# The second and the last mixture of experts: another way to choose, to invert the choice, and to add the last rows

## The chip, the cores and the metric

The kernel runs on one core of one Trainium2 chip. The time is the device time of one execution in microseconds (us); the profile is one further execution, with a trace of every instruction. TensorE is PE in the rows (PEld its weight loads), VectorE DVE, ScalarE ACT, GpSimd POOL, SyncE SP. All data is float32.

## The reference

The network adds twelve blocks, one after the other, to x (16 sequences of 64 tokens, 256 wide, so 1024 tokens): four layers, each a cross attention, a mixer and a feed-forward block. Two of the feed-forward blocks, here called mixtures, send each token to 2 of 8 experts. The last of them, cut to what matters:

```python
    logits = xt @ wg
    scores = jax.nn.softmax(logits, axis=-1)
    topv, topi = jax.lax.top_k(scores, K)                    # K = 2 of E = 8
    topv = topv / jnp.sum(topv, axis=-1, keepdims=True)
    masks = jax.nn.one_hot(topi.T, E, dtype=jnp.int32)
    locs = jnp.cumsum(masks.reshape(K * N, E), axis=0) - 1   # place within the expert
    ...
    valid = pos < capacity                                   # capacity = 256 rows an expert
    h = jax.nn.relu(jnp.einsum('ecm,emh->ech', disp, w1) + b1[:, None, :])
    y = jnp.einsum('ech,ehm->ecm', h, w2) + b2[:, None, :]
    out = jnp.sum(gate[..., None] * y[topi, pos_c], axis=1)
```

The hidden width is 1024. The second mixture (layer 1) chooses in the same way, has gelu in place of relu, adds 1e-9 to the sum of the two scores and has no capacity: every choice is kept. x in front of each block is its layer norm.

## The kernel before

X, the residual, stays in the core's memory as 8 tiles of 128 tokens by 256. `BLOCKS` calls the twelve blocks in order; `ffn1` (line 2438) is the second mixture, `ffn3` (line 2553) the last and the end of the program. `ffn0` and `ffn2` are mixtures of another kind, in which every expert sees every token.

Both `ffn1` and `ffn3` have three parts. The **front**: `norm_T` (layer norm, then transposes into xnT), the normed tokens written to a table d_x in HBM, `gate_logits` (line 2151, 16 matmuls into pgate), `softmax8`, and `ranks` (line 2178), which compares each of a token's 8 scores with each other one, 512 comparisons a partition, and counts. `choices` (line 2245) makes from the ranks one-hot tables oh of the first and second choice, and counts, by a scan and matmuls with a triangle and with ones (pq), which place each choice has within its expert. `slots` (line 2268) inverts this: for each row g*128+r of the experts' packed rows it finds the token that comes there and its weight. inb says for each of 16 groups of choices (8 tiles by 2) in which of 128 lanes each stands, val holds in which block it is times the token's number or its weight, and 16 matmuls into pi sum them up:

```python
        for j in range(J):
            self.mm(pi[:, : 2 * NG], inb[:, j], val[:, j], j == 0, j == J - 1)
```

Seven small DVE operations then make src (the row to fetch), to (the row to send to) and weight. `add_down_bias` (line 2190) adds to X the experts' output biases, weighted: it transposes the weights (pc), copies them (combT) and multiplies 9 rows by the biases downb, a matmul for each tile (pb).

The **blocks of rows**: 23 blocks of 128 rows in `ffn1` (each with its expert's weights, up and down, fetched by an indirect DMA whose row numbers are whose), 8 of 256 in `ffn3`. `take` fetches a block's tokens from d_x (xg) by an indirect DMA on the POOL queue; `expert` (line 2332) transposes them (pxg), copies (xT), multiplies (pu), applies the activation (hT), multiplies again (pd), weights the result (y) and sends it by an indirect DMA, also on the POOL queue, into a table d_y of 2048 rows, a row for each choice.

The **end**: `add_sent` (line 2371) reads d_y back in 8 DMAs of 256 KB (yk), four on SP's queue and four on ACT's. Each waits for all sends; two additions a tile put them into X. After `ffn3`, `network` writes X out in 8 DMAs on SP's queue (line 2705).

The order of instructions on each engine comes from a scheduler that goes by the program's order and by what is ready in its own estimate; `set_order(True)` with `queue` and `mm` ties instructions of an engine to the order in which they are written. In the mixtures nothing is tied before the change. Each engine works through its own instructions in order, and an indirect DMA takes its place in POOL's.

## Time and profile before

| | us |
|---|---|
| median of 3 runs | 3125.39 (3124.48 to 3126.11) |
| the profiled execution | 3139.76 |
| its span, first to last instruction | 3138.1 |
| PE busy | 2942.0 (94%) |
| DVE busy | 1966.8 (63%) |
| ACT busy | 1340.0 (43%) |
| POOL busy | 712.7 (23%) |
| last logit matmul to first expert matmul, `ffn1` | 1393.5 to 1426.5 |
| last y to the last addition to X, `ffn1` | 1612.5 to 1628.5 |
| last logit matmul to first expert matmul, `ffn3` | 2968.8 to 3001.8 |
| last y to the last addition to X, `ffn3` | 3121.5 to 3135.0 |

A row of a timeline gives the start, the duration, the engine, the line, the operation, the tiles written and read, how many, and in brackets how long the engine stood idle before it and what ended that. A row of groups gives all instructions of a kind: busy time, the mean of one in ns, and the idle time before them. Most lines of operations recorded through a queue are 72, and those of matmuls 188, so tiles are named rather than lines. A float32 matmul stands as two passes, each with a weight load. A window's row ends in the granted clock of TensorE (1 is full), the busy share of the DMA engines and GB/s.

### The profile page before, as it was taken

The numbers are of one execution on the slowest core, as the hardware profiler recorded it, in microseconds if no ns is written. First come the engines' busy times: TensorE is split into PE (matmuls) and PEld (weight loads), VectorE is DVE, ScalarE is ACT, GpSimd is POOL, SyncE is SP. The second block draws the span as 40 slices with busy tenths as digits, with TensorE's granted clock in tenths as the row PEclk, the third lists the DMA queues.
The fourth block names the chain that finished last, engine by engine and source line by source line (L and its number), as shares of the span: only waits on it lengthen the run. The fifth ranks groups of instructions, "written<-read, shape, count | busy, mean of one in ns | idle before, by whom it ended". The sixth has DMA issues, their size and how long they took to land.

```text
span 3138.1 us, 64791 instructions
## 1 busy us (share of the span) xinstructions
PE 2942.0 (94%) x27232; PEld 1792.9 (57%) x27232; DVE 1966.8 (63%) x4085; ACT 1340.0 (43%) x3013; POOL 712.7 (23%) x780
## 2 busy tenths in 40 slices
PE   8999999898999999979978999997999899998797
PEld 4666666565555554458854555544655454546676
DVE  6888886523766656961127777768874667775511
ACT  3555554412554441003325444449851255554211
POOL 1000002400210001014410100026761454541131
PEclk9999999999999999968989999998999999999789
DMA  2001000014223313017751222201111111110233
GB/s 75 32 32 32 22 29 12 18 34 109 63 79 93 99 45 82 21 55 270 296 180 52 72 72 77 65 13 44 41 57 34 60 67 55 70 44 15 95 111 120
DMA packets 73796, 223.05 MB, mean 71 GB/s; under 512 B 17457, under 2 KB 28580, under 8 KB 66594
## 3 DMA queue, kind: packets, MB, share of 16 engines
q1 hardware_dynamic: 45936, 113.99, 11.9%
q0 software_dynamic: 21840, 99.39, 9.4%
q10 hardware_dynamic: 5730, 5.53, 0.6%
q8 instruction: 215, 3.52, 0.5%
q14 instruction: 75, 0.61, 0.1%
HBM read 210.00 MB, written 12.66 MB: 71 GB/s over the span
## 4 chain that ended last, share of the span: by engine, by line
PE 81%; DVE 7%; issue 5%; POOL 2%; ACT 2%; DMA 2%; SPq 0%; POOLq 0%; ACTq 0%; DVEq 0%
PE pss L188 15%; PE o L188 13%; PE psp L188 5%; PE pu L188 5%; PE pkv L188 5%; PE pd L188 5%; PE py L188 4%; PE pst L191 4%; PE psc L188 3%; PE po L188 2%; PE pb L191 2%; PE psq L188 2%; PE psi L188 1%; PE psy L188 1%; PE pg L188 1%
## 5 line engine op out<-in xcount | busy, mean ns | idle before, releaser
L188 PE MATMUL pss<-cT,qw 128*32 128x256 f32 x8192 | 367.7, 385 | 18.8 <-ACT pr L72 18.6
L72 DVE TENSOR_REDUCE nm<-pss 128x2 f32<-128x512 f32 (+1 forms) x384 | 309.5, 862 | 83.9 <-PE pss L188 83.9
L188 PE MATMUL o<-pT,cx 128*64 128x512 f32 (+3 forms) x1088 | 351.7, 576 | 0.0
L72 ACT ACTIVATE pr<-pss,nmm 128x256 f32<-128x256 f32 x512 | 234.8, 485 | 162.2 <-DVE nmm L72 162.2
L188 PEld LDWEIGHTS pss<-cT,qw 128*32 128x32 f32 x8192 | 203.2, 109 | 148.6 <-ACT pr L72 26.3
L188 PEld LDWEIGHTS o<-pT,cx 128*64 128x64 f32 (+1 forms) x1088 | 134.2, 163 | 188.4 <-issue 161.8
L205 POOL TENSOR_SCALAR rs<-mv 128x8 f32<-128x8 f32 (+3 forms) x50 | 9.7, 195 | 1006.3 <-DVE mv L221 534.0
L72 ACT ACTIVATE pr<-pr,sm 128x256 f32<-128x256 f32 x256 | 109.1, 497 | 203.1 <-DVE sm L72 203.1
L188 PE MATMUL pkv<-wx,cT 128*128 128x512 f32 (+1 forms) x512 | 193.3, 631 | 0.6 <-issue 0.6
L72 DVE TENSOR_SCALAR pr<-pr,sm 128x256 f32<-128x256 f32 (+1 forms) x384 | 170.1, 485 | 6.6
L72 DVE TENSOR_TENSOR_SCAN h<-dA,pb 128x512 f32<-128x512 f32 x128 | 154.7, 1217 | 16.0 <-PE pb L191 9.6
L1495 POOL TENSOR_TENSOR h<-h,cb 128x1024 f32<-128x1024 f32 x64 | 151.5, 2369 | 53.6 <-DVE h L72 51.2
L2355 DVE TENSOR_SCALAR y<-pd,row 128x256 f32<-128x256 f32 x39 | 18.9, 484 | 223.2 <-PE pd L188 192.7
L72 DVE STREAM_TRANSPOSE pT<-pr 128x1024 f32<-128x1024 f32 x128 | 151.8, 1224 | 2.2
L188 PE MATMUL pd<-wd,hT 128*128 128x256 f32 x656 | 149.3, 382 | 2.9 <-DVE hT L2543 1.4
L72 ACT ACTIVATE pr<-pss,nm 128x1024 f32<-128x1024 f32 x128 | 142.7, 1115 | 11.3 <-DVE nm L72 8.7
L191 PE MATMUL pst<-ident,pr 128*128 128x128 f32 x1024 | 141.5, 281 | 5.8 <-DVE sm L72 1.9
L191 PEld LDWEIGHTS pst<-ident,pr 128*128 128x128 f32 x1024 | 110.1, 141 | 62.1 <-ACT pT L72 26.5
L72 ACT COPY pT<-pst 128x512 f32<-128x512 f32 x128 | 75.0, 586 | 164.2 <-PE pst L191 164.2
L188 PEld LDWEIGHTS pd<-wd,hT 128*128 128x128 f32 x656 | 123.1, 190 | 31.4 <-DVE hT L2543 6.2
L188 PEld LDWEIGHTS pkv<-wx,cT 128*128 128x128 f32 (+1 forms) x512 | 64.5, 189 | 118.4 <-issue 92.2
L1669 POOL TENSOR_TENSOR rnk<-rnk,mhalf 128x8 f32<-128x8 f32 (+1 forms) x84 | 130.1, 1549 | 7.0
(525 smaller groups left out, 5795.5 us busy)
## 6 DMA issues: line engine op xcount, KB each, us to landing
cT<-in_ctxT SPq DMA_DIRECT2D x32, 768.0 KB, 4.3
cx<-in_ctxP SPq DMA_DIRECT2D x32, 768.0 KB, 4.2
cT<-in_ctxT SPq DMA_DIRECT2D x32, 512.0 KB, 4.1
cT<-in_ctxT SPq DMA_DIRECT2D x64, 256.0 KB, 5.3
offb<-d_off SPq DMA_DIRECT2D x16, 576.0 KB, 3.7
cb<-d_C SPq DMA_DIRECT2D x16, 512.0 KB, 4.1
wu<-in_L_ffn_w POOLq DMA_DIRECT2D x8, 1024.0 KB
wd<-in_L_ffn_w POOLq DMA_DIRECT2D x8, 1024.0 KB
```

Of the source, the lines that this page charges most:

```text
L72: ins = getattr(self.engine, op)(*args, **kwargs)
L188: self.in_order(self.nc.tensor.matmul(out, lhsT=lhsT, rhs=rhs, start=start, stop=stop))
L191: self.in_order(self.nc.tensor.transpose(out, in_, self.ident))
L205: nc.gpsimd.tensor_scalar(t[:p, :n], in_, scale, eps, ALU.mult, ALU.add)
L1495: nc.gpsimd.tensor_tensor(hs[i], hs[i], cbs[hf, g], ALU.mult)
L1669: nc.gpsimd.tensor_tensor(r, r, self.mhalf[:, : n * H], ALU.pow)
L2355: nc.vector.tensor_scalar(y[:, i, :], po[:, i * D : (i + 1) * D], weight[:, g + i : g + i + 1], None, ALU.mult)
```

## The change

It has four parts, in both mixtures.

- `choose` takes the place of `gate_logits`, `softmax8`, `ranks` and `choices`: the first choice by the maximum of the logits, the second by the maximum of what is left, ties to the lower expert through a falling row 8 to 1. The exponentials are not divided by their sum; `over_both` divides at the end. A one-element Exp stands ahead of the logits.
- `slots`: val becomes the loaded operand, 32 columns wide, and inb the moving one; output j goes to the 32 rows 32*(j%4), and a matmul with fold adds the four parts up. The token's row comes first (pi), its fetch is issued, and only then the products for the weight and for the row to send to are made on POOL and multiplied (pw). The experts' biases are multiplied in four groups of rows (pc, pb; downb now stands four times, at rows 0, 32, 64 and 96). Several operations move from DVE to POOL, and the order is tied.
- `add_sent`: the last block of rows is not sent. The read-back comes ahead of the last block in the program, on SP's queue alone, and waits for the other sends; POOL adds the two halves. hits is 1 where a token is the one that a row of the last block belongs to; 8 matmuls with it add the last y. d_y is now cleared in `ffn1` too (2 MB), and the last expert of `ffn3` is worked in two blocks of 128.
- the output DMAs alternate between SP and ACT.

The instructions' order on each engine is otherwise that of before. On POOL in `ffn1` it is now: comb, comb, up, down, at, up, val, down, up, xg, gate, xg, val, val, down, xg; in `ffn3`: kept, kept, comb, at, val, xg, xg, gate, xg, val, val, xg. On PE: pq, pn (`ffn1`), pc, pi, the first fold product, pb, pw, pxg, two fold products, pu. On DVE the first addition of a yk stands ahead of the last y.

```diff
-        self.downb = self.const.tile([9, 3, D], F32, name="downb")
-        nc.scalar.dma_start(out=self.downb, in_=a["downb"])
+        self.downb = self.const.tile([P, 3, D], F32, name="downb")
+        for q in range(4):
+            nc.scalar.dma_start(out=self.downb[32 * q : 32 * q + 9], in_=a["downb"])
...
+    def choose(self, wg, d_x, one, mid):
...
+        nc.scalar.activation(best[:, 3, 0:1], self.xn[:, 0, 0:1], AF.Exp)
...
+        self.set_order(True)
...
+        dve.tensor_reduce(best[:, 0], pg3, AX.X, ALU.max)
+        dve.tensor_tensor(d, pg3, bc(best[:, 0], 2, 8), ALU.subtract)
+        nc.scalar.activation(p, d, AF.Exp)
+
+        dve.scalar_tensor_tensor(w, d, 0.0, falling, ALU.is_ge, ALU.mult)
+        dve.tensor_reduce(best[:, 1], w, AX.X, ALU.max)
+        dve.tensor_tensor(by_t[:, 0], w, bc(best[:, 1], 2, 8), ALU.is_equal)
+        dve.scalar_tensor_tensor(d, by_t[:, 0], -4.0, p, ALU.mult, ALU.add)
+        dve.tensor_reduce(best[:, 2], d, AX.X, ALU.max)
+        dve.tensor_tensor(w, d, bc(best[:, 2], 2, 8), ALU.is_equal)
+        dve.tensor_tensor(w, w, falling, ALU.mult)
+        dve.tensor_reduce(best[:, 1], w, AX.X, ALU.max)
+        dve.tensor_tensor(by_t[:, 1], w, bc(best[:, 1], 2, 8), ALU.is_equal)
...
+        pool.tensor_tensor(at[:, :, :NG], at[:, :, :NG], at[:, :, 1:], ALU.subtract)
+        spot = self.spot.rearrange("p k t -> p (k t)")
+        pool.tensor_tensor(val[:, 0, :, :NG], at[:, :, :NG], bc(spot, 2, NG), ALU.mult)
...
+        def inverted(ps, k):
+            for j in range(J):
+                q = j % 4
+                self.mm(ps[32 * q : 32 * q + 32, :], val[:, k, j, :], inb[:, j], j < 4, j >= J - 4)
...
+        inverted(pi[:, :P], 0)
+        rows = one.tile([P, 3, P], F32, name="rows")
+        dve.tensor_copy(rows[:, 0], pi[:, :P])
+        pf = mid.tile([P, 512], F32, tag="m", name="pf")
+        self.mm(pf[:, :32], rows[:, 0], self.fold)
+        src, to = (one.tile([P, NG], I32, name=f"at{k}") for k in range(2))
+        dve.tensor_copy(src, pf[:, :NG])
+        got = taken(src)
+
+        pool.tensor_tensor(gate, gate, bc(r, 1, 2), ALU.mult)
+        pool.tensor_tensor(val[:, 1, :, :NG], at[:, :, :NG], bc(gate.rearrange("p k t -> p (k t)"), 2, NG), ALU.mult)
+        pool.tensor_tensor(val[:, 2, :, :NG], at[:, :, :NG], bc(self.token, 2, NG), ALU.mult)
...
+            for q in range(4):
+                rg = slice(32 * q, 32 * q + 9)
+                self.mm(pb[q // 2][:, q % 2, k, :], cT[rg, k, :], self.downb[rg, i, :])
+        pw = mid.tile([P, 2, P], F32, tag="m", name="pw")
+        for k in range(2):
+            inverted(pw[:, k, :], 1 + k)
+        act.copy(rows[:, 1:], pw)
+        for k in range(2):
+            self.mm(pf[:, 32 + 32 * k : 64 + 32 * k], rows[:, 1 + k], self.fold)
...
+    def add_sent(self, d_y, sent, last, src, g, row, one, pool, mid):
...
+        nc.vector.tensor_copy(own, src[:, g : g + 1])
+        nc.vector.tensor_scalar(hits, row, own, None, ALU.is_equal)
...
+            ins = nc.sync.dma_start(out=yk, in_=d_y.rearrange("(k t p) d -> t p k d", t=NT, p=P)[t])
             for other in sent:
                 self.tc.add_manual_dep(ins.ins, other, sync, reason="sent rows")
+            nc.gpsimd.tensor_tensor(yk[:, 0], yk[:, 0], yk[:, 1], ALU.add)
+            yks.append(yk)
+        y = last()
+        for t in range(NT):
+            nc.vector.tensor_tensor(self.X[:, t, :], self.X[:, t, :], yks[t][:, 0], ALU.add)
+        for t in range(NT):
+            ps = mid.tile([P, 512], F32, tag="m", name="py")
+            self.mm(ps[:, :D], hits[:, t * P : (t + 1) * P], y[:, 0, :])
+            nc.vector.tensor_tensor(self.X[:, t, :], self.X[:, t, :], ps[:, :D], ALU.add)
...
-        tc.nc.sync.dma_start(out=out[t * P : (t + 1) * P, :], in_=n.X[:, t, :])
+        (tc.nc.sync, tc.nc.scalar)[t % 2].dma_start(out=out[t * P : (t + 1) * P, :], in_=n.X[:, t, :])
```

## The prediction

> **What bounds the kernel now.** I read the clock and span first (one core, mean granted TensorE clock 0.952), then the chain of work that ended last: TensorE holds 81% of it. So only stretches in which TensorE has little to do can be shortened by this change. The view of stretches, cut to the fronts and ends of the second mixture (ffn1, rows 1 and 2) and the last (ffn3, rows 3 and 4), shows them. Columns: stretch, length, busy time of PE, PEld, DVE, ACT, POOL, granted clock, DMA share, GB/s.
>
> ```profile
> 1389.00:1426.00 37.00, 22.00 (x88) 18.00 (x87) 20.20 (x64) 3.41 (x4) 9.73 (x10) 0.53 0.48 171
> 1612.00:1632.00 20.00, 0.44 (x2) 0.04 (x1) 8.81 (x28) 0.00 (x0) 2.23 (x3) 0.61 0.47 145
> 2965.00:3002.00 37.00, 22.42 (x97) 18.48 (x98) 19.51 (x59) 0.84 (x2) 7.28 (x8) 0.54 0.44 135
> 3121.00:3138.00 17.00, 0.48 (x3) 0.07 (x1) 6.30 (x17) 0.00 (x0) 0.98 (x1) 0.63 0.55 188
> ```
>
> In all, 111 us, and in none of them the experts' weights are multiplied. The timeline of the last mixture's front tells what follows what (start, length, engine; x32 means 16 matmuls, since each f32 matmul stands as two passes):
>
> ```profile
> 2968.81 0.23 DVE L2157 COPY s<-pgate 128x64 f32<-128x64 f32 x1 [2.85 <-PE pgate L188]
> ...
> 2970.62 0.69 DVE L2184 TENSOR_TENSOR gt<-s 128x512 f32<-128x512 f32 x1
> ...
> 2979.46 2.50 DVE L2296 TENSOR_TENSOR inb<-sl,lane 128x512 f32<-128x512 f32 x4
> ...
> 2982.68 7.04 PE L188 MATMUL pi<-val,inb 128*128 128x32 f32 x32 [6.57 <-DVE val L2304]
> ...
> 2990.84 1.08 POOL L2324 DMA_INDIRECT xg<-L_ffnx,at  x1 [21.03 <-DVE at L2314]
> ...
> 2992.81 7.16 PE L188 MATMUL pb<-downb,combT 9*128 9x256 f32 x16 [1.40 <-DVE combT L2198]
> ...
> 3001.80 9.14 PE L188 MATMUL pu<-xT,wu 128*128 128x256 f32 x32 [0.78 <-DVE xT L2341]
> ```
>
> Logits end at 2968.8, the first expert matmul (pu) starts at 3001.8: 33.0 us of a serial chain. In ffn1 the same chain goes from 1393.5 to 1426.5, also 33.0. The end of ffn1, from its timeline:
>
> ```profile
> 1612.48 0.48 DVE L2355 TENSOR_SCALAR y<-pd,row 128x256 f32<-128x256 f32 x1 [7.91 <-PE pd L188]
> 1613.24 0.98 POOL L2358 DMA_INDIRECT L_ffny<-y,at  x1 [7.39 <-DVE y L2355]
> ...
> 1615.78 2.23 SPq L2377 DMA_DIRECT2D yk<-L_ffny  x4
> ...
> 1621.52 1.22 DVE L2384 TENSOR_TENSOR X<-X,yk 128x256 f32<-128x256 f32 x3 [5.68 <-DMA yk<-L_ffny]
> ```
>
> The last y waits for its send, the sends for the read-back, the read-back for the sums; X is whole at 1628.5, 16.0 us after that y. In ffn3 it is 3121.5 to 3135.0, with the output's own 3.1 us behind it.
>
> **The change, step by step.** Times count from the logits' end.
>
> *Choice.* The copy, softmax and pairwise ranks (five 0.69 us operations on 512 elements) go; eleven DVE operations on 64 elements at 0.26 (row s<-pgate and its neighbours, with the gap), the scan (0.45) and prev (0.30) stay on the path: 3.6 us. Before, prev ended 6.5 later in ffn3 and 7.8 in ffn1, where an activation table load of 1.28 us stood in the chain; the new tiny Exp on xn makes it early, while ScalarE idles. Gain 2.9 and 4.2. In ffn1 15 instead of 8 logit matmuls now stand behind the last transposes; at the 0.18 us a pass of that row's cold part this ends them 1 to 2.6 us later: -1.5.
>
> *Inversion (pi).* Before, 16 matmuls load 128 columns and move 32 or 46: 7.06 us. After, val (32 columns) is loaded and inb moves, four column groups side by side. The nearest row is pss in the attention, 128x32 loads, 8192 passes in 367.7 us, 45 ns each at 256 columns; half of those use two row groups as well (64 passes in 1.96 us, 31 ns), which leaves 59 ns for the plain kind, against 0.23 us for a full-width pass (pd, 16 in 3.72). At half clock and half the columns that is 59 ns again: 32 passes, 1.9 us. Here a rule has to be weighed. These two stretches are pi and pb in ffn1:
>
> ```profile
> 1411.00:1418.00 7.00, 6.79 (x32) 6.79 (x32) 0.16 (x1) 1.28 (x1) 0.53 (x1) 0.50 0.89 362
> 1418.00:1425.00 7.00, 7.00 (x18) 5.19 (x17) 3.77 (x14) 0.00 (x0) 4.38 (x5) 0.50 0.33 87
> ```
>
> The granted clock is 0.50 in both, though PE is busy for all 14 us. The Trainium skill, "TensorE: Matmul & The Clock Gate", Part 1, lets about 3.4 us of sustained work restore full clock; by it the new pi, pb and pw would run mostly at full clock and take about half of the 7.7 us I give them, some 3 us more gain per mixture. The row decides: thin products left the clock low, so I price all of the front at half clock. Its page "TensorEngine Tiling (Array Packing)", under Key Properties, says that changing the tiling mode drains TensorE; the front now changes it about five times. No row shows a price; the attention changes modes with no idle time in front, so between 0 and 0.5 us in all, taken as 0.
>
> *New work on POOL.* The subtraction at and the three val products move to GpSimd, beside comb. Nearest rows, and the issue costs that stand between them on this in-order queue:
>
> ```profile
> L1095 POOL TENSOR_TENSOR tapp<-tapp,tapb 128x256 f32<-128x256 f32 x16 | 11.7, 730 | 70.1 <-ACT tapp L72 69.0 <-DVE tapb L72 1.1
> L1016 POOL TENSOR_TENSOR xd<-xt,dt 128x512 f32<-128x512 f32 x8 | 10.4, 1298 | 9.6 <-ACT xt L72 9.5
> ```
> ```profile
> 1407.04 1.10 POOL L2488 DMA_INDIRECT up<-in_L_ffn_up,whose  x1 [12.45 <-DVE whose L2480]
> 1408.44 1.45 POOL L2488 DMA_INDIRECT down<-in_L_ffn_down,whose  x1 [0.30 <-issue]
> 1410.20 1.32 POOL L2488 DMA_INDIRECT up<-in_L_ffn_up,whose  x1 [0.30 <-issue]
> ```
>
> 368 elements (ffn1) take 0.98 by interpolation, 256 (ffn3) 0.74; a gather issue is 1.0 to 1.45 plus 0.30. The rule against this: "GPSIMD Engine Reference", 4.1, puts elementwise work on VectorE because GpSimd is about twice as slow with two inputs, and section 7 adds 50% for reads whose step is over 8 bytes (at is read beside 24-wide rows, spot and gate as broadcasts). DVE's own val rows were 0.53 (ffn1) and 0.42, so row and rule agree on the factor; with the surcharge five POOL operations cost about 2.5 us more in ffn1 and 1.5 in ffn3. I take the rows and keep the surcharge for the range.
>
> *ffn3 front.* After prev (3.6): oh, place, slots, low 3.35 us and inb 2.5, so 5.85; before 6.6. POOL is free and has val by then, so pi runs with inb and ends 0.6 later (before 7.9 after inb). Copy 0.29, fold product 0.4, conversion 0.17, gaps: src 1.0 later, the first gather issue at 3.6+7.8. Three gathers (1.25 each), gate 0.2, and two val products bring POOL to 13.4; pw, 64 passes, 3.8 us from the first of them at 12.6, to 16.4; only then pxg (1.1), two fold products (0.8), pu at 18.3. So 21.9 instead of 33.0: +11.1. Row-packed pb (16 passes, about 2 us), two 1.2 us additions to X and hits (0.69) lie under the POOL stretch; without it they would cost 3 us.
>
> *ffn1 front.* Here the POOL queue is in the way. After prev, pn, nine small operations to whose (4.0), place, sums and reciprocal: inb would be whole at 9.75. But POOL stands comb (needs the reciprocal, 5.5), up, down, at, up, val in that order: val comes at 11.8. pi ends at 13.7, src 14.7, gather 14.8 (behind a second down and up), gate, gather, val twice to 19.6, pw to 22.3, pxg and folds, pu at 23.8. Before, pu was 25.2 after prev. Gain 4.2-1.5+1.4: +4.1.
>
> *Ends.* The last block's y is no longer sent: eight products with the one-hot hits (2 passes of 0.23 each, 3.7 us) add it. The seven other reads wait only for the block before, whose y is 8.4 us earlier (1604.1 to 1612.5 before). Sent 0.8 after it, landed 2.2 later, the read-back is issued 5.1 us ahead of the last y, 256 KB eight times on SP alone; in ffn1 it took 10.3 us before, in ffn3 7.7. POOL adds pairs at 0.74. In ffn1 the first sum stands ahead of the last y on DVE and holds it for 1 to 2 us; X is whole 7 us after the last product instead of 16, but the next norm's statistics now stand behind all sums (-1): +8. In ffn3 X is whole 4.8 after it instead of 13.5: +8.7, say 8.9 with the outputs on two queues; but the last expert is cut in two blocks of 8.2 us instead of one of 14.7: -1.9. Net +7.0.
>
> *Costs at nothing.* 2 MB of zeros in ffn1 go out at 1384, over 20 us ahead of the first gather of tokens; uncovered 5 us. The start has three more small loads ahead of X[4..7] and a few constants; DVE waits for POOL until 10.3 there and those tiles are needed later. numbers, comb, val memsets replace combT and lane on POOL (about +0.7), but in ffn3 the 0.96 weight issue now comes after rstd: even.
>
> Sum: 11.1+4.1+8+7.0 = 30.2 of the profiled 3139.8 (span 3138.1 and 1.7 around it), so 3109.6; the runs' median is 0.9954 of that: **3095 us**, a gain of 1.0%.
>
> **Rivals.** *POOL turns into the bound of the fronts*: if its products and issues cost 1.1 us more each, about 8 us go: 3103; the in-order queue speaks for it, the rows above against. *The ends don't overlap*: one queue reads slower (ffn1's first landing took 5.7 us), or POOL's sums and the in-order DVE hold y, so that only a third of 15 us is won: 3105. *It goes better*: full clock early and cheap packed products, 38 us: 3087. *Slower*: GpSimd's small operations cost as its power does (rnk, 8 elements, 1.67 us) or more; fourteen stand on the paths, so it decides from 2.2 us extra each; at 2.5, 3130. Against it: its add and multiply rows. *Nothing won*: fronts and ends hidden by weights that land later; DMA is only half busy there.
>
> **How the numbers follow.** This theory 0.52, POOL 0.18, ends 0.13, better 0.09, nothing 0.03, slower 0.05. Own range of the likeliest 3087 to 3104; with surcharge, drains and the rivals of the same sign 3080 to 3116. Faster by over 0.2% (6 us, about what runs of this kernel can tell apart) 0.92, within it 0.03, slower 0.05.
>
> **What would show it.** Right: pu 20 to 24 us after the logits in ffn3 and about 30 in ffn1; pi under 3 us; yk issued before the last y; X whole within 8 us. Wrong: POOL products above 2 us, pw waiting for val beyond that, a read-back that starts after the last y.

## The result, and the profile after

The changed kernel takes 3114.12 us (median of 14 runs, 3099.45 to 3122.83). The kernel before, run beside it, takes 3136.12 (14 runs, 3124.48 to 3144.13): its three runs of 3125.39, on which the prediction was put, were among its quicker ones. The ratio is 0.9933, 95% interval 0.9918 to 0.9948, a gain of 22 us (16 to 26). Forecast were 3095 and a gain of 30.

The profiled execution took 3099.45, its span is 3097.8 at a granted clock of 0.964. That is 40 us below the profile of before, so almost half of the difference between the two profiles is not the change's. The view of stretches shows where it lies: 40 us of the stage before the second mixture, where both kernels have the same code. Columns as before: stretch, length, PE, PEld, DVE, ACT, POOL, granted clock, DMA share, GB/s. First the kernel before:

```profile
1320.00:1360.00 40.00, 40.00 (x390) 23.94 (x388) 32.20 (x55) 5.17 (x9) 0.00 (x0) 0.54 0.00 1
```

The same stretch of the changed kernel:

```profile
1320.00:1360.00 40.00, 37.65 (x458) 25.92 (x458) 35.93 (x68) 5.25 (x9) 1.41 (x3) 0.91 0.05 15
```

PE is busy for all 40 us in the first and does fewer matmuls (390 against 458), at 0.54 of the clock against 0.91. Up to the start of the last addition to X ahead of `ffn1` the execution of before took 1385.6 us, the one of after 1367.4. Every time below that is compared between profiles is therefore one of a stage, or the time from that addition to the end ("from ffn1 on"): 1752.4 before, 1730.3 after, a gain of 22.1, as the timed runs have it. The stages are taken from the traces' starts and ends, those of an addition or a y from its start; differences are taken before rounding:

| stage, us | before | after | gain | forecast |
|---|---|---|---|---|
| `ffn1`, last addition to X to last logit | 7.9 | 10.8 | -2.9 | -1.5 |
| `ffn1`, last logit to pu | 33.0 | 28.6 | 4.4 | 5.6 |
| `ffn1`, last y to the next transposes | 19.7 | 12.3 | 7.4 | 8 |
| `ffn3`, last logit to pu | 33.0 | 23.4 | 9.6 | 11.1 |
| `ffn3`, y of block 13 to y of block 15 | 14.7 | 17.5 | -2.8 | -1.9 |
| `ffn3`, last y to the end | 16.5 | 11.2 | 5.4 | 8.9 |

The stretches of fronts and ends in the changed kernel, the same view:

```profile
1378.30:1406.90 28.60, 11.62 (x143) 8.79 (x143) 16.72 (x48) 2.29 (x4) 14.22 (x18) 0.54 0.68 263
1593.20:1605.50 12.30, 4.54 (x17) 2.75 (x17) 9.86 (x27) 0.00 (x0) 5.94 (x8) 0.88 0.60 169
2942.70:2966.10 23.40, 13.35 (x143) 8.38 (x143) 14.11 (x35) 1.00 (x3) 11.28 (x16) 0.53 0.47 156
3086.60:3097.80 11.20, 4.26 (x16) 2.79 (x16) 6.69 (x17) 0.00 (x0) 5.35 (x7) 0.84 0.62 207
```

In the fronts (rows 1 and 3) PE is now busy for 11.6 and 13.4 us where it was for 22, still at half the clock (0.54, 0.53); POOL's time rose from 9.7 to 14.2 and from 7.3 to 11.3. In the ends (rows 2 and 4) PE has work, the products with hits, at 0.88 and 0.84.

The timeline of the last mixture's front (start, length, engine, line, operation, tiles, count, idle time before it and what ended that):

```profile
2942.67 0.23 DVE L72 TENSOR_REDUCE best<-pgate 128x8 f32<-128x64 f32 x1 [3.56 <-PE pgate L2283]
...
2946.23 0.29 DVE L72 TENSOR_TENSOR prev<-upto,oh 128x128 f32<-128x128 f32 x1
...
2951.52 2.41 PE L205 MATMUL pi<-inb,val 128*32 128x128 f32 x32 [1.39 <-POOL val L72]
...
2955.47 1.12 POOL L72 DMA_INDIRECT xg<-L_ffnx,at  x1 [4.01 <-DVE own L2493]
...
2959.96 4.08 PE L205 MATMUL pw<-inb,val 128*32 128x128 f32 x64 [2.96 <-POOL val L72]
...
2965.16 0.37 ACT L72 COPY rows<-pw 128x256 f32<-128x256 f32 x1 [14.59 <-PE pw L205]
...
2966.06 7.15 PE L205 MATMUL pu<-xT,wu 128*128 128x256 f32 x32
```

The choice takes 3.9 us from the logits to the end of prev (3.6 forecast), pi 2.4 in place of 7. The first gather of tokens is issued 12.8 us after the logits instead of 22. Then pw waits for val from POOL, and its result is copied 5.2 us after its first pass.

In `ffn1` another wait ends last. Its timeline, cut to the first gather of tokens, pw and the transposes of the tokens (pxg):

```profile
1397.96 0.95 POOL L72 DMA_INDIRECT xg<-L_ffnx,at  x1 [2.13 <-DVE own L2493]
...
1401.20 3.60 PE L205 MATMUL pw<-inb,val 128*32 128x128 f32 x64 [1.71 <-POOL val L72]
...
1405.97 0.41 PE L2439 MATMUL pxg<-ident,xg 128*128 128x128 f32 x2 [1.17 <-DMA xg<-L_ffnx,at]
```

pw's result is there at 1405.1, but the tokens land only 8.0 us after their gather was issued (the DMA engines are busy for 0.98 of that time, and the gathers of three up and two down blocks were issued ahead of it), and TensorE waits 1.2 us for them. pu follows 0.9 us later. So in `ffn1` the gather's issue, which stands in POOL's queue, and its landing set the end of the front, not pw.

The timeline of the last end:

```profile
3082.50 4.15 SPq L2498 DMA_DIRECT2D yk<-L_ffny  x8
...
3085.49 0.72 POOL L2501 TENSOR_TENSOR yk<-yk 128x256 f32<-128x256 f32 x1 [4.81 <-DMA yk<-L_ffny]
...
3086.59 0.48 DVE L2455 TENSOR_SCALAR y<-pd,row 128x256 f32<-128x256 f32 x1
...
3090.83 2.42 POOL L2501 TENSOR_TENSOR yk<-yk 128x256 f32<-128x256 f32 x3 [0.17 <-DMA yk<-L_ffny]
...
3094.62 0.42 DVE L2509 TENSOR_TENSOR X<-X,py 128x256 f32<-128x256 f32 x1
```

The read-back is issued 4.1 us ahead of the last y, and its first tile is summed before that y. But the last tiles land 4.5 us behind y (3091.1 by the packets), three POOL sums follow them in a row, and the last addition ends at 3095.0, 8.45 after the start of y. DVE has little room in this time: 15 of its 16 additions start behind y, and it is busy with them for 6.2 of the 8.0 us up to their end. In `ffn1` the same view shows more of an overlap:

```profile
1588.02 3.97 SPq L2498 DMA_DIRECT2D yk<-L_ffny  x8
...
1593.18 0.48 DVE L2455 TENSOR_SCALAR y<-pd,row 128x256 f32<-128x256 f32 x1 [1.42 <-PE pd L205]
...
1600.16 0.74 DVE L2509 TENSOR_TENSOR X<-X,py 128x256 f32<-128x256 f32 x2
```

5.2 us ahead there, X whole 7.7 after y, and y was not held: it follows the y before it by 8.4, as before.

### The profile page after: what moved, and what is told of

Its sections match the earlier page's. It is cut to its first block, busy times and chain, and to the rows that moved or that the text cites. A ratio compares the mean times of both kernels' runs of the same rounds, so it can differ in the third digit from the quotient of the medians.

```text
span 3097.8 us, 65295 instructions
## 1 busy us (share of the span) xinstructions
PE 2926.3 (94%) x27452; PEld 1779.4 (57%) x27452; DVE 1962.2 (63%) x4058; ACT 1343.7 (43%) x3027; POOL 733.3 (24%) x817
## 3 DMA queue, kind: packets, MB, share of 16 engines
q1 hardware_dynamic: 47536, 115.57, 12.1%
## 4 chain that ended last, share of the span: by engine, by line
PE 81%; DVE 12%; ACT 2%; POOL 2%; issue 2%; DMA 1%; SPq 0%; DVEq 0%; POOLq 0%; ACTq 0%
PE pss L205 15%; PE o L205 13%; PE pu L205 8%; PE pd L205 7%; PE psp L205 6%; PE pkv L205 5%; PE py L205 4%; PE pst L208 4%; PE po L205 2%; PE pb L208 2%; PE psq L205 2%; PE psy L205 1%; PE pg L205 1%; DVE nm L72 1%; PE ptk L208 1%
## 5 line engine op out<-in xcount | busy, mean ns | idle before, releaser
L72 ACT ACTIVATE pr<-pss,nm 128x1024 f32<-128x1024 f32 x128 | 142.7, 1115 | 11.2 <-DVE nm L72 8.6
L205 PE MATMUL py<-h,ident 128*128 128x512 f32 x256 | 130.9, 597 | 0.0
```

The lines of the kernel that those rows point to most:

```text
L72: ins = getattr(self.engine, op)(*args, **kwargs)
L205: self.in_order(self.nc.tensor.matmul(out, lhsT=lhsT, rhs=rhs, start=start, stop=stop))
```

## The experiments

Each is timed beside the kernel before on the same chip; e1 to e4, e5 to e8 and e9 to e12 ran on three different ones, so ratios are compared across them. What they gave, with the profiled stages (us); "pu" is from the last logit to the first pu, "end" in `ffn1` from the last y to the next transposes, in `ffn3` from the start of block 13's y to the end of the program:

| kernel | ratio to before (95%) | from ffn1 on | pu `ffn1`, `ffn3` | end `ffn1`, `ffn3` |
|---|---|---|---|---|
| before | 1 | 1752.4 | 33.0, 33.0 | 19.7, 31.2 |
| changed | 0.9933 (0.9918 to 0.9948) | 1730.3 | 28.6, 23.4 | 12.3, 28.7 |
| e1 | 0.9962 (0.9936 to 0.9988) | 1742.7 | 28.6, 23.4 | 19.9, 31.3 |
| e2 | 0.9982 (0.9960 to 1.0004) | 1745.9 | 31.7, 33.1 | 11.2, 29.5 |
| e3 | 0.9926 (0.9903 to 0.9948) | 1727.9 | 27.8, 23.3 | 12.0, 28.4 |
| e4 | 0.9945 (0.9923 to 0.9967) | 1732.3 | 28.9, 23.5 | 11.9, 30.5 |
| e5 | 0.9892 (0.9858 to 0.9926) | 1729.1 | 29.7, 25.3 | 11.4, 28.7 |
| e6 | 0.9913 (0.9881 to 0.9945) | 1726.7 | 29.5, 23.4 | 11.5, 29.8 |
| e7 | 0.9898 (0.9862 to 0.9935) | 1729.2 | 29.1, 23.3 | 11.5, 29.4 |
| e8 | 0.9916 (0.9884 to 0.9949) | 1727.6 | 28.8, 23.7 | 13.3, 29.5 |
| e9 | 0.9880 (0.9841 to 0.9919) | 1722.8 | 29.3, 22.8 | 12.1, 25.8 |
| e10 | 0.9866 (0.9830 to 0.9903) | 1712.8 | 23.3, 20.7 | 12.2, 28.5 |
| e11 | 0.9926 (0.9900 to 0.9951) | 1731.8 | 29.7, 23.4 | 12.2, 28.4 |
| e12 | 0.9903 (0.9869 to 0.9936) | 1727.2 | 27.5, 24.8 | 11.9, 26.7 |

The column "from ffn1 on" has in it a stage that no edit touches, from the transposes behind `ffn1` to the last addition to X ahead of `ffn3`: it took 1328.3 us before and 1328.4 after, but 1323.1 (e10) to 1333.1 (e1) in the others. Differences of that size in this column mean nothing by themselves.

**e1, the fronts alone.** The end of the mixtures and the output's queue are those of before.

```diff
-    def add_sent(self, d_y, sent, last, src, g, row, one, pool, mid):
+    def add_sent(self, d_y, sent, pool):
...
-            ins = nc.sync.dma_start(out=yk, in_=d_y.rearrange("(k t p) d -> t p k d", t=NT, p=P)[t])
+            ins = (nc.sync, nc.scalar)[t % 2].dma_start(
+                out=yk, in_=d_y.rearrange("(k t p) d -> t p k d", t=NT, p=P)[t]
+            )
...
-            self.expert(xg[:, :1], 1, *rest, 14, d_y, sent, big, mid, two, 2)
...
+                self.expert(xg, 2, *rest, 2 * e, d_y, sent, big, mid, two, 2)
+            self.add_sent(d_y, sent, two)
```

> The changed kernel with the old ends: every block sent, read back by SP and ACT after the last send, two additions a tile, the last expert of the last mixture in one block of 256, outputs on SP. Theory (the gain is the sum of stages read from the two profiles): the fronts alone win 33.0-28.6 in the second mixture less about 3 us by which its logits end later, 33.0-23.4 in the last plus 2 us in its first blocks, about 12 us in all against the kernel before. Its profile should show logits to pu at 28.6 and 23.4 us, and the ends as before: y to the next norm's transposes 19.7 us, last y to the end 16.6 us. Rival (the profiles differ by 40 us, so the fronts also gain in stages outside the mixtures): 25 us or more. Rival (the fronts win nothing because the weights land later anyway): under 3 us.

**e2, the ends alone.** The choice, the inversion and the bias product are those of before (the edit is shown against the changed kernel).

```diff
-    def choose(self, wg, d_x, one, mid):
+    def choices(self, r, one, mid):
...
-    def slots(self, place, oh, r, gate, comb, val, i, NG, one, big, mid, taken):
+    def slots(self, place, oh, s, one, mid, NG, keep):
```

> The kernel before with only the new ends (last block not sent, read-back during it, one-hot product, last expert in two blocks, outputs on two queues, d_y cleared in the second mixture). Theory: y to the next norm's transposes 12.3 instead of 19.7 us in the second mixture (+7.4), in the last one y13 to y15 17.5 instead of 14.7 (-2.8) and last y to the end 11.2 instead of 16.6 (+5.4): 10 us in all. Rival (the prediction's own figure): 15 us, with the split at -1.9 and the last end at +8.9. Rival (the ends don't overlap): 4 us or less.

Measured 3124.2 for e1 and 3132.1 for e2, gains of 0.38% and 0.18%; together 0.56%, where the whole change has 0.67% (0.52 to 0.82). e2's interval reaches no gain at all, so the times show only that the parts add up within their noise. The stages show more: with the new fronts alone pu comes at 28.6 and 23.4, with the new ends alone the ends are 8.5 and 1.7 us shorter. The parts don't get in each other's way in them, and the weak one is the end of `ffn3`.

The later logits of `ffn1` belong to the ends, not to the fronts. In the kernel before and in e1, 16 of the 32 logit passes stand behind the last transposes; in every kernel with the new ends, e2 with the old front too, it is 30. The kernel before, then e2:

```profile
1390.57 2.94 PE L188 MATMUL pgate<-wg,xnT 128*128 128x8 f32 x16 [0.68 <-DVE xnT L196]
```
```profile
1396.44 6.41 PE L188 MATMUL pgate<-wg,xnT 128*128 128x8 f32 x30
```

The new ends put the clearing of d_y and the row of numbers ahead of this norm, and the order that the scheduler chose changed with them; which of the two did it was not tried apart. The 30 passes took 6.4 us at a granted clock of 0.50 (changed kernel, e2) and 4.6 at 0.72 (e8, e9), so the whole stage came to 10.8 and 11.7 or to 8.4 and 8.5 us, against 7.9 and 7.5 with 16.

**e3, POOL's products on VectorE.** In the gathers' shadow the products for weight and row are DVE's; in `ffn1` also at and the first val.

```diff
-        pool.tensor_tensor(at[:, :, :NG], at[:, :, :NG], at[:, :, 1:], ALU.subtract)
+        first = dve if NG > 16 else pool
+        first.tensor_tensor(at[:, :, :NG], at[:, :, :NG], at[:, :, 1:], ALU.subtract)
...
-        pool.tensor_tensor(gate, gate, bc(r, 1, 2), ALU.mult)
-        pool.tensor_tensor(val[:, 1, :, :NG], at[:, :, :NG], bc(gate.rearrange("p k t -> p (k t)"), 2, NG), ALU.mult)
-        pool.tensor_tensor(val[:, 2, :, :NG], at[:, :, :NG], bc(self.token, 2, NG), ALU.mult)
+        dve.tensor_tensor(gate, gate, bc(r, 1, 2), ALU.mult)
+        dve.tensor_tensor(val[:, 1, :, :NG], at[:, :, :NG], bc(gate.rearrange("p k t -> p (k t)"), 2, NG), ALU.mult)
+        dve.tensor_tensor(val[:, 2, :, :NG], at[:, :, :NG], bc(self.token, 2, NG), ALU.mult)
```

> The changed kernel with the gate and the two later val products on VectorE, and in the second mixture also the subtraction and the first val product. Theory A (POOL's queue of products and gather issues sets when pw can start): pw starts about 3 us sooner in the last mixture and 2 us sooner in the second, where pi also starts 2 to 3 us sooner; logits to pu about 20 instead of 23.4 and about 24.5 instead of 28.6 us; 6 to 8 us faster than the changed kernel. Theory B (pu waits for the tokens to land, or the products are slow by the clock): pw starts sooner, pu at most 1 us sooner, under 2 us in all.

The products shortened (0.54 and 0.43 us on DVE for 0.82 and 0.62 on POOL) and no longer stood behind the gathers: pw began 2.9 us after the copy of pi's result, where it had been 4.7 in `ffn1` and 6.0 in `ffn3`. Yet pu came 0.8 sooner in `ffn1` and 0.2 in `ffn3`. The timeline of e3's last front tells what took the time:

```profile
2960.20 3.75 PE L205 MATMUL pw<-inb,val 128*32 128x128 f32 x61
...
2967.87 0.37 ACT L72 COPY rows<-pw 128x256 f32<-128x256 f32 x1 [14.02 <-PE pxg L2440]
```

61 of the 64 passes stand in one stretch of 3.75 us, and the last begins 4.7 us after the first (3.7 in the changed kernel), but their result came 7.7 us after the first instead of 5.2; in `ffn1` 8.9 instead of 3.9. So a new delay took the place of POOL's.

**e4, the last expert of `ffn3` undivided.** Both of its blocks stay unsent, and each tile gets two products.

```diff
-            self.mm(ps[:, :D], hits[:, t * P : (t + 1) * P], y[:, 0, :])
...
+            for i in range(G):
+                self.mm(ps[:, :D], hits[:, i, t * P : (t + 1) * P], y[:, i, :], i == 0, i == G - 1)
...
-            self.expert(xg[:, :1], 1, *rest, 14, d_y, sent, big, mid, two, 2)
...
-                lambda: self.expert(xg[:, 1:], 1, *rest, 15, d_y, None, big, mid, two, 2),
+                lambda: self.expert(xg, 2, *rest, 14, d_y, None, big, mid, two, 2),
```

> The changed kernel with the last expert of the last mixture in one block of 256 again, neither half sent: the read-back waits only for the expert before, and 16 products with two one-hot tables add both halves. Theory (the split cost 2.8 us and the read-back of 2 MB, 9.6 us from its issue, ends after the last y): y13 to y15 14.7 instead of 17.5 us, all yk added before the last y, X whole 8 to 8.5 us after the last y because 32 passes at 0.23 stand there, end 11 after it: about 3 us faster than the changed kernel. Rival (the split is free and the end is bound by the outputs): within 1 us. Rival (products at a lower clock cost double): 4 us slower.

The end became 1.8 us longer, not shorter. Its timeline:

```profile
3080.99 2.65 DVE L2507 TENSOR_TENSOR X<-X,yk 128x256 f32<-128x256 f32 x3 [0.62 <-POOL yk L2503]
...
3083.57 0.47 DVE L2455 TENSOR_SCALAR y<-pd,row 128x256 f32<-128x256 f32 x1
3084.09 5.13 PE L205 MATMUL pd<-wd,hT 128*128 128x256 f32 x16 [4.92 <-DVE y L2455]
```

The y of block 14 stood behind seven additions of yk on the in-order DVE, each waiting for a POOL sum, and pd of block 15 waited 4.9 us for that y. This is the wait that the rival "the ends don't overlap" named; in the changed kernel it doesn't arise, because only one y is left by then.

**e5, the bias sum later.** e3, with the addition of pb to X behind the conversion of the rows.

```diff
-        for h in range(2):
-            X = self.X.rearrange("p (k q) d -> p q k d", k=2)[:, 2 * h : 2 * h + 2]
-            dve.tensor_tensor(X, X, pb[h], ALU.add)
...
         dve.tensor_tensor(to, row, none, ALU.add)
+        for h in range(2):
+            X = self.X.rearrange("p (k q) d -> p q k d", k=2)[:, 2 * h : 2 * h + 2]
+            dve.tensor_tensor(X, X, pb[h], ALU.add)
```

> As the run with the products on VectorE, with the two additions of pb to X moved behind the seven small operations on pf, so that VectorE reads nothing while pw runs. In that run pw took 8.9 and 7.7 us from its first pass to the copy of its result, against 3.9 and 5.2 in the changed kernel. Theory A (VectorE's PSUM reads of pb, which fell into pw, slow it): pw back to 4 to 5.5 us, pu's first pass 2 to 4 us after the logits sooner than there, less the 1.2 us by which the first addition now holds pu's PSUM buffer. Theory B (pw is slow because it follows pb without a pause, whatever VectorE does): pw stays at 7.5 to 9 us and logits to pu at 23 to 25 and 28 to 29.5 us.

pw's result came 8.7 and 7.5 us after its first pass, as in e3. An overlap of DVE's additions with pw is therefore not what delays it. pu came later than in the changed kernel (29.7 and 25.3), as it now begins 0.1 us behind the end of the first of those additions.

**e6, undivided, with an order.** e4, with the order tied: y of block 14 ahead of the additions of yk.

```diff
-            nc.vector.tensor_scalar(
+            self.queue("dve", nc.vector).tensor_scalar(
...
+            if then is not None and i < n - 1:
+                then()
...
+            self.set_order(True)
+            y = last(read)
+            self.set_order(False)
```

> As the run with the last expert undivided and neither half sent, with VectorE's order fixed: y14, then the eight additions of yk, then y15. In that run y14 stood behind seven additions that waited for the read-back, and y13 to y15 took 20.4 us. Theory: y13 to y15 falls to about 14.7, X whole 7.3 and the end 10 us after the last y: 24.8 from y13 to the end, against 28.7 in the changed kernel, so 4 us faster than it. Rival (the read-back takes TensorE's or the weights' share of memory and the undivided block is slow by itself): y13 to y15 above 17.

The end is 29.8, 0.7 better than e4 and still behind the changed kernel. The tie put all of PE in the program's order too, and each group of pu now waits for the activation before it, as the timeline shows:

```profile
3079.95 1.13 PE L205 MATMUL pu<-xT,wu 128*128 128x256 f32 x4 [0.56 <-ACT hT L2449]
```

**e7, undivided, first half sent.** Only block 15 is left out of the sends; the read-back follows the send of block 14.

```diff
-            if sent is None:
+            if sent is None or then is not None and i == n - 1:
                 continue
...
+            if then is not None:
+                then()
...
-            self.expert(xg[:, :1], 1, *rest, 14, d_y, sent, big, mid, two, 2)
...
+                lambda then: self.expert(xg, 2, *rest, 14, d_y, sent, big, mid, two, 2, then),
```

> The changed kernel with the last expert of the last mixture in one block of 256, its first half sent, its second half added by the product; the read-back waits for the first half. This takes away the split alone. Theory: y13 to y15 14.7 instead of 17.5; the read-back is issued about 0.7 us ahead of the last y instead of 4.1, so X is whole some 10 us after it (8.5 in the changed kernel) and the end is 12.6 after it: 27.3 from y13 to the end instead of 28.7. If the split cost only the predicted 1.9, y13 to y15 would be 15.6.

The timeline of its end:

```profile
3098.51 4.15 SPq L2502 DMA_DIRECT2D yk<-L_ffny  x8
...
3099.25 0.48 DVE L2455 TENSOR_SCALAR y<-pd,row 128x256 f32<-128x256 f32 x1 [3.81 <-PE pd L205]
...
3104.56 5.04 POOL L2505 TENSOR_TENSOR yk<-yk 128x256 f32<-128x256 f32 x6 [1.25 <-DMA yk<-L_ffny]
```

From the y of block 13 to that of block 15 it takes 14.7 us again, so the division costs 2.8. But the read-back now starts 0.7 us ahead of the last y, X is whole 12.0 after it, and the end is 29.4 against 28.7. The division buys the early read-back, and is worth slightly more than it costs.

**e8, the read-back on two queues.** The odd tiles on ACT's queue behind the last activation, and every addition to X behind the last y.

```diff
-            ins = nc.sync.dma_start(out=yk, in_=d_y.rearrange("(k t p) d -> t p k d", t=NT, p=P)[t])
+            ins = (nc.sync, nc.scalar)[t % 2].dma_start(
+                out=yk, in_=d_y.rearrange("(k t p) d -> t p k d", t=NT, p=P)[t]
+            )
...
+            self.tc.add_manual_dep(ins.ins, self.last_act.ins.name, after, reason="behind the last activation")
...
+            self.tc.add_manual_dep(first.ins, self.last_y.ins.name, after, reason="behind the last y")
```

> The changed kernel with half of the read-back on ACT's queue behind the last activation, and the additions of yk behind the last y. Theory (one queue keeps the DMA engines only 0.66 to 0.82 busy during the last read-back, at 203 to 252 GB/s, against 0.99 and 338 with two queues in the kernel before): the last read lands about 2 us sooner than 9.6 us after the first issue, X whole 6.5 to 7.5 us after the last y instead of 8.5. Rival (the sums on GpSimd and VectorE's sixteen additions set the pace): X whole at 8 us or later. In the second mixture X was whole 7.7 us after the last y, with VectorE busy all the time; there no gain under either, or a loss of up to 1 us since no addition stands ahead of y now.

No gain: both ends are 0.8 to 1.0 us longer, X is whole 9.6 us after the last y of `ffn3` (8.45 before the edit), and the packets of the read-back ended 4.8 us behind that y (4.5). The second queue could begin only after the last activation, and by then the first was well under way. The edit also moved the additions that used to run ahead of y behind it, and the two effects were not tried apart. Of the 9.6 us behind y, DVE's 16 additions at 0.42 are 6.7.

**e9, undivided, with y first and nothing else tied.** e6 with one tie in place of the order: the additions of yk behind the y of block 14.

```diff
-        if G > 1:
-            self.set_order(True)
-            y = last(read)
-            self.set_order(False)
...
+                ins = nc.vector.tensor_tensor(self.X[:, t, :], self.X[:, t, :], yks[t][:, 0], ALU.add)
+                if G > 1:
+                    self.tc.add_manual_dep(ins.ins, self.last_y.ins.name, after, reason="behind y")
```

> As the undivided last expert with neither half sent, but the eight additions of yk stand behind y14 on VectorE and nothing else is fixed; in the last attempt the fixed order made pu wait for the activations (12 us instead of 7). From the runs so far: the read-back is issued about 4 us after y13 and takes 8.9 us to its last landing, so the additions end about 14.5 us after y13. Theory: y13 to y15 14.7 to 15.5 us, the end 10.1 after it (32 passes, 7.3): 25 to 25.6 from y13 to the end instead of 28.7, 3 to 4 us faster than the changed kernel. Rival (the additions still hold y15 or its products): 28 or more.

The timeline of its end:

```profile
3077.73 0.48 DVE L2455 TENSOR_SCALAR y<-pd,row 128x256 f32<-128x256 f32 x1 [9.90 <-PE pd L205]
3078.14 5.08 DVE L2511 TENSOR_TENSOR X<-X,yk 128x256 f32<-128x256 f32 x8
3083.14 0.47 DVE L2455 TENSOR_SCALAR y<-pd,row 128x256 f32<-128x256 f32 x1
```

All eight additions of yk fit between the two y's; the read-back no longer ends behind the last y at all, and X is whole 7.3 after it. But they hold the last y: from block 13's y to it, 15.8 us pass instead of 14.7. The end is 25.8 us against 28.7, so 2.8 of the 4.4 that were missing there came back. Median 3096.48.

**e10, the bias products first.** e3, with pb multiplied as soon as its operand is there, ahead of pi.

```diff
         act.copy(cT, pc)
+        pb = [big.tile([P, 2, 2, D], F32, tag="b", name="pb") for _ in range(2)]
+        for k in range(2):
+            for q in range(4):
+                rg = slice(32 * q, 32 * q + 9)
+                self.mm(pb[q // 2][:, q % 2, k, :], cT[rg, k, :], self.downb[rg, i, :])
...
-        pb = [big.tile([P, 2, 2, D], F32, tag="b", name="pb") for _ in range(2)]
-        for k in range(2):
-            for q in range(4):
-                rg = slice(32 * q, 32 * q + 9)
-                self.mm(pb[q // 2][:, q % 2, k, :], cT[rg, k, :], self.downb[rg, i, :])
```

> As the run with the products on VectorE, with the bias products pb put ahead of pi, where TensorE is idle; pw then follows pi and the first fold product. In the earlier two runs pw followed pb at once and took 8.9 and 7.7, then 8.7 and 7.5 us, against 3.9 and 5.2 behind a pause of 1.7 to 3 us in the changed kernel. Theory A (pw is slow when it follows pb at once): pw 4 to 5.5 us here and pu 3 to 5 us sooner after the logits than in the changed kernel (about 24.5 and 20 us). Theory B (it is slow whenever TensorE has had no pause of some us before it): 7 us or more again and no gain. Theory C (the gathers' traffic slows it): slow in the second mixture alone.

The timeline of its front in `ffn1`:

```profile
1409.57 3.64 PE L205 MATMUL pw<-inb,val 128*32 128x128 f32 x64 [0.93 <-DVE val L72]
...
1413.28 0.37 ACT L72 COPY rows<-pw 128x256 f32<-128x256 f32 x1 [9.75 <-PE pw L205]
```

pw's result came 3.7 us after its first pass in both mixtures, and pu at 23.3 and 20.7, 5.3 and 2.8 us sooner than in the changed kernel. In `ffn3` this is pw's sooner result. In `ffn1` TensorE still waits for the tokens (0.9 us, until 1415.4); the gather is issued 16.2 us after the logits instead of 19.7, since the subtraction and the first val product no longer stand ahead of it in POOL's queue, and lands after 6.1 us instead of 8.0. e3 has the same sooner gather, but there the late pw held pu. e10 has both edits, and e3, with only one of them, shows that moving the products alone doesn't bring it; pb ahead of pi with the products left on POOL was not run.

Median 3100.03; the upper end of the ratio's interval, 0.9903, lies below the lower end of the changed kernel's first interval (0.9918), though not of its second (0.9900 in e11). Of the 17.5 us that e10's profile is shorter from `ffn1` on, 8.0 are the two fronts; 5.3 lie in the stage between the mixtures, which no edit touches, and 2.3 in the logits of `ffn1`.

**e11, the changed kernel once more**, with no edit, to see what one kernel differs by between two profiles.

> The changed kernel once more, as it is, beside the next one. It tells what of a difference between two profiles is the kernel's and what the run's: the stages from the second mixture's logits on should agree with the first profile of the changed kernel within 0.5 us (28.6, 12.3, 23.4, 17.5, 11.2), while the time up to the second mixture, 1367.4 in that profile and 1385.6 in the one of the kernel before, may be anything from 1367 to 1391. If that early time differs by kernel and not by run, it is 1367 to 1372 again.

The early stretch of this execution:

```profile
1320.00:1360.00 40.00, 40.00 (x440) 24.17 (x440) 32.87 (x56) 5.93 (x10) 0.70 (x1) 0.63 0.00 1
```

A clock of 0.63 where the other profile of the same kernel had 0.91. It reached the last addition ahead of `ffn1` after 1380.0 us, the other after 1367.4, and from there on took 1731.8, the other 1730.3. Two executions of one kernel thus differ by 12.6 us ahead of `ffn1`, where the first two profiles differ by 18. pw's result took 3.95 and 5.2 us, as in the first profile. The stages agree within 0.4 us but for one: pu came at 29.7 instead of 28.6 in `ffn1`, because the tokens landed later there. So a difference of 1 us in that column, such as e3's 0.8, is within what one kernel shows.

**e12, e9 and e10 together.**

```diff
-        pool.tensor_tensor(at[:, :, :NG], at[:, :, :NG], at[:, :, 1:], ALU.subtract)
+        first = dve if NG > 16 else pool
+        first.tensor_tensor(at[:, :, :NG], at[:, :, :NG], at[:, :, 1:], ALU.subtract)
...
+        pb = [big.tile([P, 2, 2, D], F32, tag="b", name="pb") for _ in range(2)]
...
+                lambda then: self.expert(xg, 2, *rest, 14, d_y, None, big, mid, two, 2, then),
```

> Both findings together: products on VectorE with pb ahead of pi, and the last expert undivided with neither half sent. Theory (the stages are independent): logits to pu 23.3 and 20.6 us, y13 to the end 25.8; 5.3, 2.8 and 2.9 us sooner than the changed kernel, 11 us in all, about 3103 beside 3114. Rival (the sooner start of the experts' products meets weights that have not landed): the stage behind pu grows by what the front won.

The end of `ffn3` kept most of its gain (26.7), but pw's result took 8.3 and 8.4 us although the front has the instructions of e10. The timeline:

```profile
1395.63 3.64 PE L205 MATMUL pw<-inb,val 128*32 128x128 f32 x64 [0.93 <-DVE val L72]
...
1403.95 0.37 ACT L72 COPY rows<-pw 128x256 f32<-128x256 f32 x1 [14.30 <-remote]
```

and the stretches of the 64 passes and of the time behind them:

```profile
1395.60:1399.70 4.10, 3.64 (x64) 2.96 (x64) 3.36 (x4) 0.00 (x0) 3.19 (x4) 0.50 0.96 395
1399.70:1403.10 3.40, 0.00 (x0) 0.00 (x0) 0.00 (x0) 0.00 (x0) 2.52 (x3) 1.00 1.05 397
```

The passes are recorded at the usual pace, then nothing is recorded on TensorE for over 3 us at a granted clock of 1.00, and then the result is there. Median 3102.47, beside 3112.74 for e11 on the same chip. The intervals of e9, e10 and e12, six runs each, overlap with one another and with e11's, so which is best, and how much any of them gains over the changed kernel, is read from the stages alone.

## Why the prediction was right or wrong

**Right: the sign, where the gain comes, and the wide range.** The gain comes where the sum put it: e1 and e2 show both parts, and the time between the mixtures is level (1328.3 us before, 1328.4 after). 3114 lies in 3080 to 3116, at its upper edge, and misses the range of the likeliest. Of the 19 us by which it misses 3095, 10.7 are the foot on which the sum was set (median of before 3125.39 of three runs, 3136.12 of fourteen); some 8 are a gain of 22 in place of 30. The stages of the table gained 21.0 of the 30.2: 5.0 are missing in the ends, 2.7 in the fronts, 1.4 in the logits.

**The step that was mis-sized: the end of `ffn3`.** It was put at +7.0 net and gave 2.6 (5.4 less 2.8). "X is whole 4.8 after" the last y became 8.45. The read-back was issued 4.1 instead of 5.1 us ahead of y, and took 8.6 instead of 7.7 us to land (one queue moved the 2 MB at some 275 GB/s, counted from its first packet; the two queues of before together at 322), so that it ended 4.5 us behind y instead of 2.6: 1.9 us. Behind that landing came 3.95 us of POOL's last sums and DVE's additions, where 2.2 were counted: 1.75 us. The additions alone put 4.8 out of reach: 15 of them stand behind y, 6.2 us of DVE's time, and even in e9, where the eight of yk are done by then, X is whole only after 7.3. The division of the last expert cost 2.8, not 1.9; e7 shows this by leaving it out (14.7). The rival "the ends don't overlap" named about the right size for this mixture (2.6 of 7.0 won) and was wrong for `ffn1`; e9, which gives the read-back one more y to hide under, took 2.8 us back.

**The end of `ffn1`** was +8 and gave 7.4. The forecast that the first sum holds the last y for 1 to 2 us fell: y came 8.4 after the one before it, as it had. The next norm did start later behind X (4.6 instead of 3.7 us, the -1 of the sum).

**The front of `ffn3`** was +11.1 and gave 9.6. Counted from prev, the first gather is issued after 8.95 us (7.8 forecast), val is done after 13.95 (13.4), pw's result is there after 18.6 (16.4) and pu begins after 19.5 (18.3). The worst step is pw (5.2 us to its result, 3.8 counted). Another was counted at nothing: DVE and POOL slow each other. Two lines of `ffn1`'s front in the changed kernel, then one of e10's:

```profile
1388.78 3.60 DVE L72 TENSOR_TENSOR inb<-sl,lane 128x512 f32<-128x512 f32 x4
...
1390.38 0.84 POOL L72 TENSOR_TENSOR at<-at 128x368 f32<-128x368 f32 x1
```
```profile
1404.39 2.49 DVE L72 TENSOR_TENSOR inb<-sl,lane 128x512 f32<-128x512 f32 x4
```

The inb operation during which POOL subtracts takes 1.72 us, the last one 0.68; e10 has that subtraction and the first val product on DVE, and there all four take 0.68 to 0.69. In `ffn3`, where both stay on POOL in every kernel with the new front, the four take 3.23 us instead of the 2.5 of the sum. That is on the path, as pi goes along with inb.

**The front of `ffn1`** was +5.6 without the logits and gave 4.4. POOL's queue had been laid out to within 1.1 us: val after 11.4 us (11.8 forecast), the first gather after 15.9 (14.8), the last val product after 19.8 (19.6). pi's 32 passes took 1.93 us, as priced from pss, but its result could be copied only 3.0 after val. pw's result was there after 23.1 (22.3) and pu began after 24.8 (23.8). The sum let pu follow pw and counted no landing of the gathered tokens; in the trace these landed 8.0 us after their issue, behind pw's result, and pu followed them. The -1.5 for later logits was right in its count (15 instead of 8 matmuls behind the last transposes) and cost 2.9 us at the clock of this execution; it comes with the new ends (e2), not with the new front (e1).

**The rules weighed.** The row was right about the clock: the fronts ran at 0.53 and 0.54 of it for 23 and 29 us, and the extra gain that the Trainium skill ("TensorE: Matmul & The Clock Gate", Part 1) would have given didn't come. A change of the tiling mode left no gap between records where one could be seen (pf starts at 2954.34 for 0.63 us, pb at 2954.91), so nothing speaks against 0 there; the late results of pw below stay unexplained. On GpSimd ("GPSIMD Engine Reference", 4.1 and 7) both were too dear here: the products took 0.82 and 0.62 us, against 0.98 and 0.74 from the rows, 1.5 times VectorE's time. The page's surcharge is for an innermost step of over 8 bytes; in these reads that step is 4 bytes or 0, so it didn't bear on them. The one read of POOL with a long innermost step (kept from oh, 64 bytes) took 0.43 us beside 0.32 for the next product of the same size. Neither row nor rule counted what POOL's products cost DVE meanwhile.

**POOL as the bound** was given 0.18, at 3103, a gain of 22, and the measured gain is 22; by the number alone the result fits this rival, or that of the ends (3105), better than the theory. The stages decide otherwise: its mechanism, products and issues dearer by 1.1 us each, didn't occur, and the fronts lack 2.7 us, not 8. POOL's place does bound the fronts: pw waits for val from POOL in `ffn3`, the tokens' gather stands behind POOL's products in `ffn1`, and in e10, without that, pu is 2.8 and 5.3 us sooner. But that place was in the sum at nearly its price; it is gain left lying, and a small part of the shortfall. Slower, nothing won, and better didn't occur.

**What stays open** is pw. Its result came 3.3 to 5.2 us after its first pass in every kernel with the products on POOL, 3.7 in e10, and 7.5 to 8.9 in e3, e5 and e12. None of the suspected causes fits all of these: pb doesn't stand just ahead of pw in e12, DVE doesn't add to X meanwhile in e5, and the gathers are the same in e10 and e12. In all six late cases (both mixtures of e3, e5 and e12), and in none of the others, a stretch of 3.4 us at full clock begins around pw's last recorded pass, with half clock behind it, and the result is copied only near its end (0.4 us ahead of it to 1.0 behind). A rise alone doesn't delay pw: in the changed kernel's `ffn3` it comes 0.65 us ahead of the copy. And in e12 the result was overdue before the rise: e10's copy comes 0.5 us behind the last pass, while in e12 the clock rises only 0.9 and 1.6 us behind it. So the rise didn't start the delay there; what did stays open.

## What to carry to other kernels

Moving a read-back ahead of the last block pays only as far as that block is long: count issue, landing at one queue's rate and every sum behind it against the block's time, see what additions stay behind the last y wherever it lands, and hide it under one more block before dividing one (e9 against e4 and e7). On in-order engines a tie for the one instruction that others wait for is enough; a tie of everything lost most of it (e6 ends 3.9 us behind e9). Where POOL issues gathers, put the one that is waited for ahead of products and of weights that are not needed yet: in `ffn1` its issue and landing set the front's end. That last order is argued from the traces; of it only e10's part, the products off POOL, was run. Before two profiles are compared, take the stages that the change doesn't touch out of the difference: here 18 of 40 us lay in one, and another moved by up to 10 us from kernel to kernel.

## What the runs showed of the hardware

- The stage ahead of `ffn1`, in which DVE is busy for 31 to 38 of 40 us, holds a stretch at a granted clock of 0.50 in every trace, 6.8 us long (changed kernel, e4) to 58 us (e2), 47.8 in the kernel before; the time up to `ffn1` went from 1367 to 1391 us with it and with other differences between runs. The same kernel had 6.8 in one profile and 34.1 in the next.
- The record of a matmul's passes can end several microseconds before its result is there: 5 us in e12's pw, where the last of 64 recorded passes starts at 1398.85 and the copy of the result at 1403.95.
- GpSimd's float32 multiplications of 256 and 368 elements a partition took 0.62 and 0.82 us beside VectorE's 0.43 and 0.54, a factor of 1.5; an indirect DMA's issue held it for 0.94 to 1.45 us and another 0.16 to 0.30 behind it, more than a product.
- DVE's operations with both operands in SBUF, the core's working memory, slowed down while POOL worked; those with one operand in PSUM, where TensorE leaves its results, didn't. In the changed kernel's trace, additions of yk to X took up to 0.97 us beside POOL's sums and 0.41 to 0.43 without them; additions of py, from PSUM, took 0.41 to 0.42 in both cases. inb took 1.72 and 1.10 us in place of 0.68, and POOL's val beside inb 0.94 in place of 0.62. e10, with POOL's two operations beside `ffn1`'s inb moved away, has 0.68 to 0.69 there again.
- An indirect gather of 128 rows of 1 KB landed 8.0 us after its issue in `ffn1`, behind five gathers of weight blocks and with the DMA engines busy for 0.98 of the time, and 2.9 us after it in `ffn3` of e9.
